# A four-layer vision network on one core: the first layer's group norm and layer norm move to the scalar engine, its input comes in channels first, and the gates' silu is spread

## The chip, the cores and the metric

The kernel runs on one core of a Trainium2 chip. A core has a matrix engine (TensorE, PE in the profile), a vector engine (VectorE, DVE), a scalar engine (ScalarE, ACT), GpSimd (POOL), and SyncE (SP), whose queue issues the DMAs here. Each engine works through its own list of instructions in order and waits on semaphores for the others. The metric is the device time of one execution in microseconds; it was 7655.37 us, the median of three runs (7653.72 to 7661.91).

## The reference, cut to what matters

Four images of 64 x 64 tokens with 128 channels pass through four residual layers. The change touches only the first, a selective scan in four directions over a group-normalized image.

```python
x = x + _L0_conv_ref(_gn(x), ...)          # the changed layer; three more follow

def _ss2d_forward(x, ...):                 # x is group-normalized, B x 64 x 64 x 128
    xz = x @ in_proj_w.T
    xh, z = jnp.split(xz, 2, axis=-1)      # 256 channels each
    z = jax.nn.silu(z)                     # the gate
    xc = conv_general_dilated(transpose(xh), conv_w, 'SAME', feature_group_count=DI)   # depthwise 3 x 3
    xc = jax.nn.silu(xc + conv_b)
    xs = the image row by row, column by column, and both reversed      # K = 4 directions
    delta, Bs, Cs = ...                    # small projections of xs
    h = exp(delta * A) * h + (delta * u) * B     # per channel and per state n = 0..15, along 4096 tokens
    y = sum over the directions of (C * h summed over n), plus D * xs
    y = (y - mean) / sqrt(var + EPS) * out_norm_w + out_norm_b          # layer norm over 256 channels
    return (y * z) @ out_proj_w.T
```

`_gn` is a group norm with 32 groups of 4 channels: mean and variance over the image and the 4 channels of a group.

## The kernel before, in words

**The scan loop.** `layer0` works through 128 units: 4 images (b = 0 to 3), for each 4 directions k, for each direction 8 chunks c of 512 tokens. So units 0 to 31 belong to image 0, 32 to 63 to image 1, 64 to 95 to image 2 and 96 to 127 to image 3. A unit has 16 slots, one per state n. In each of the 2048 slots

- GpSimd makes `dB = du * B` for both halves of the 256 channels (L689, one 128x1024 product; three buffers),
- ScalarE makes `dA = exp(delta * A)` twice, once for each half (L694), into PSUM (three buffers, `psx`),
- VectorE runs two scans `h = dA * h + dB` (L695),
- TensorE transposes a quarter of an older group of four states (L542: eight transposes into the single PSUM buffer `pt`), ScalarE copies that to SBUF (`hT`, L552), and TensorE multiplies it with C into `yT` (L577).

ScalarE's list in a slot is dA, (place act0), dA, (place act1), hT, (place act2). VectorE's list is (place dve), scan, scan, and what falls due of `yT`. TensorE's is the transposes of this slot, the products of the slot before, then one side step. These four engines keep the order that the Python code writes (`manual_schedule`); SP's DMAs are placed by the framework.

**What a unit does besides.** In fixed slots (`TABLE`) it prepares the next unit: x projections and their copies `xd` and `Ct` (slot 7), `delta` by Exp and Ln on ScalarE and one VectorE operation (slots 8 and 10), `du` on GpSimd twice. Near slots 5 and 7 `y` is added up (L593), with `ln_st` statistics in direction 2.

**The side work.** Two generators are cut into steps by `yield`, and the loop takes a step when its due time has come and the slot number is in `SIDE[need]`; `SPACE` keeps the side path free for so many slots afterwards. `later(place, f, slots=n)` queues a piece for a place n slots on.

- `before(b)` prepares the next image while the current one is scanned. For each of 8 chunks it loads 512 tokens (`l`), transposes them on TensorE (`m`, L317) and takes `bn_stats` on VectorE from PSUM (L318). After `group_scale` it loads each chunk again, transposes it again (`x`, L336), and VectorE writes the normalized values `x * s + o` from PSUM into a padded tile `xn` of 10 rows of 66 (L635 through `later`): 8 rows for this chunk, and one row each for the neighbours' borders. GpSimd clears the borders (L182, L322, L332). Then follow two gates (`z`: a product on TensorE, L177, and a silu), and, one chunk behind, two convolutions of nine taps (`c`, L159), one tap in each slot from 11 on to slot 3 of the next unit.
- `after(b)` finishes an image while the next is scanned (for image 3, in its own last units). For each of 8 chunks: load y and z, `ln_mv` on VectorE (L389), ln of the variance on ScalarE, then at step `n` the factor `nb` (L396) and four VectorE operations `normed` of 128x256 in the next slot (L423); two steps `m` with four transposes each (L404) and ScalarE's copy `yg` with the norm's weights; at `g` the product with z on GpSimd (L412); the output projection (L417), and the residual on VectorE (L426).
- `silu` is Exp, Ln(1+e), Exp on ScalarE, then one product on VectorE and a store (L358, L359). For a convolution the three are one slot apart; for a gate all three are in one slot (act0, act1, act2) and the product comes in the next.

`rest` finishes the two last chunks of image 0's convolutions in the first units, and `opening` prepares image 0. The small PSUM tiles of the side work share one bank (`spare`).

Of the kernel before, what the change touches and what calls it, by code (L numbers as in the profile page):

```python
# [11 lines left out]
F32 = mybir.dt.float32  # L12
AF = mybir.ActivationFunctionType
ALU = mybir.AluOpType
# [3 lines left out]
P = 128  # L18
# [3 lines left out]
DM = 128  # L22
NJ = NT // P
CH = 512
NCH = NT // CH
K4 = 4
WD = 32 * 129 * 16
NS = 16
# [54 lines left out]
def layer0(sh, A, x_in, x_out, scr, ahead):  # L83
# [7 lines left out]
    with ExitStack() as ctx:  # L91
# [57 lines left out]
            nc.vector.tensor_tensor(tap, tap, w_in[:, s : s + 1, :].to_broadcast([P, 9, P]), ALU.mult)  # L149
        tiles = lambda ap: ap.rearrange("(q p) d -> p q d", p=P)  # L150

        def conv(xn, s, bank):
# [13 lines left out]
            return pm  # L166
# [6 lines left out]
        def gates(b, c, v, bank, later, es=(None, None)):  # L173
            for s in range(2):
                yield "z"
                zp = bank("zp")
                nc.tensor.matmul(zp, lhsT=w_in[:, 2 + s, :], rhs=v, start=True, stop=True)  # L177
                silu(zp, 0.0, 0.0, scr(f"z{b % 3}")[s, :, c * CH : (c + 1) * CH], later, (("act1", 1), ("act2", 1), 2), es[s])

        def rows():  # L180
            xn = tmp.tile([P, 10, 66], F32, name="xn", bufs=3)
# [3 lines left out]
        def opening(bank, steps):  # L185
# [49 lines left out]
            scaled = []  # L235
# [32 lines left out]
            for c in range(DENSE + 1):  # L268
                if c < DENSE:
                    if c + 2 < NCH:  # L270
                        scale(c + 2)
                    xn = padded(c)
                    pm = psy.tile([P, 2, 2 * P], F32, name=f"yT{c % 2}").rearrange("p r d -> p (r d)")
                    acc = depthwise(c)
                if last:
                    grown(0, c - 1, 0, last[0], soon, pair("e")[:, 0], gathers[0])
                    grown(0, c - 1, 1, last[1][:, 0], soon, last[1][:, 1], gathers[1])
                if c < DENSE:
                    for _ in gates(0, c, xg[:, 8 * c : 8 * c + 8], bank, soon):
                        pass  # L280
                    for _ in conv(xn, 0, lambda name: pm):
# [16 lines left out]
        def rest(tiles, bank, later):  # L298

            for c, xn in enumerate(tiles, DENSE):  # L300
                for s in range(2):
                    pm = yield from conv(xn, s, bank)
                    grown(0, c, s, pm, later)

        def before(b, bank, later):

            st = small.tile([P, NCH, 6], F32, name="gn_st")
            for c in range(NCH):  # L310
                yield "l"
                t = tmp.tile([P, 4, DM], F32, name="xs", tag="t2", bufs=4)
                nc.sync.dma_start(t, tiles(x_in(b)[c * CH : (c + 1) * CH, :]))
                yield "m"
                pt = bank("gn_ps")
                for q in range(4):
                    nc.tensor.transpose(pt[:, q * P : (q + 1) * P], t[:, q, :], sh.ident)  # L317
                later("dve", lambda c=c, pt=pt: nc.vector.bn_stats(st[:, c, :], pt))  # L318
            yield "m"
            s_, o_ = sh.group_scale(st, psm, small, "m", exp_rstd)  # L320
            xn, ahead = None, rows()
            nc.gpsimd.memset(ahead[:, 0, :], 0.0)  # L322
            for c in range(NCH + 1):
                behind, xn = xn, ahead
                if c < NCH:
                    yield "l"
                    t = tmp.tile([P, 4, DM], F32, name="xt", tag="t2", bufs=4)
                    nc.sync.dma_start(t, tiles(x_in(b)[c * CH : (c + 1) * CH, :]))
                    if c < NCH - 1:
                        ahead = rows()  # L330
                    else:
                        nc.gpsimd.memset(xn[:, 9, :], 0.0)  # L332
                    yield "x"
                    pt = bank("x_ps")
                    for q in range(4):
                        nc.tensor.transpose(pt[:, q * P : (q + 1) * P], t[:, q, :], sh.ident)  # L336
                    grid = pt.rearrange("p (h w) -> p h w", w=64)
                    parts = [(xn[:, 1:9, 1:65], grid)]
                    if c > 0:
                        parts.append((behind[:, 9:10, 1:65], grid[:, 0:1]))  # L340
                    if c < NCH - 1:
                        parts.append((ahead[:, 0:1, 1:65], grid[:, 7:8]))
                    for dst, src in parts:
                        later("dve", nc.vector.tensor_scalar, dst, src, s_, o_, ALU.mult, ALU.add)
                    yield from gates(b, c, xn[:, 1:9, 1:65], bank, later)
                if c == 0:
                    continue
                for s in range(2):
                    pm = yield from conv(behind, s, bank)
                    grown(b, c - 1, s, pm, later)  # L350

        def silu(v, bias, minus, dst, later, wait, e=None):

# [21 lines left out]
        def after(b, st, later, bands):  # L375

            for c in bands:
# [14 lines left out]
                later("act1", nc.scalar.activation, rs, mv[:, :, 1], AF.Ln, bias=sh.eps5)  # L392
                yield "n"

                nb = spare("nb")[:, 0:4]
                nc.scalar.activation(nb, rs, AF.Exp, scale=-0.5)  # L396
                for q in range(4):
                    later("dve", normed, y[:, q, :], mv[:, q, 0:1], nb[:, q : q + 1])
                yg = tmp.tile([P, 2, CH], F32, name="yg", bufs=2)
                for s in range(2):  # L400
                    yield "m"
# [20 lines left out]
        def normed(y, mean, factor):  # L422
            nc.vector.scalar_tensor_tensor(y, y, mean, factor.to_broadcast([P, 2 * P]), ALU.subtract, ALU.mult)  # L423

        def residual(b, rows, xr, op):
            nc.vector.tensor_tensor(xr, xr, op, ALU.add)  # L426
# [128 lines left out]
        def products(G, q, hT):  # L555
# [64 lines left out]
            m={0, 1, 2, 4, 5, 11, 12, 13, 14, 15},  # L620
            x={0, 1, 4, 5, 11, 12, 13, 14, 15},
            n={0, 1, 2, 3, 4, 11, 12, 14, 15},
            z={0, 1, 2, 3, 4, 11, 12, 13, 14, 15},
            c={11},
            g={7},
            f=(),
            l=(),
        )
        SPACE = dict(m=1, x=1, n=1, z=2, c=3, g=0)
        todo = {}  # L630
        slot = 0

        def later(place, f, *a, slots=1, **kw):

            todo.setdefault((slot + slots, place), []).append(lambda: f(*a, **kw))  # L635
# [3 lines left out]
                f()  # L639

        def flush_all():
            for at in range(slot, slot + 6):
                for place in ("dve", "act0", "act1", "act2"):
                    flush(place, at)

        with tc.manual_schedule(engines=order):
            idle = lambda: None
            left = opening(any_bank, [idle, fetched, idle, begun, grown_steps, readied])
            u, ready, bd, Wd, Bb = (got[n] for n in ("u", "ready", "bd", "Wd", "Bb"))
            sides.append(Side(rest(left, spare, later), 18 * len(left), 0, 2 * NS * len(left)))  # L650
            for i, (b, k, c) in enumerate(units):
                if i % per == 0:
                    ln_st = small.tile([P, NJ, 1, 6], F32, name="ln_st")
                    first = len(left) if b == 0 else 0
                    if b + 1 < NB:
                        sides.insert(len(sides) if b == 0 else 0, Side(before(b + 1, spare, later), 17 + 8 * 22, NS * (i + first), (28 - first) * NS))
                first_out = i > 0 and rev
                rev = k >= 2
                pos = orders[b].index(k)
# [17 lines left out]
                for n in range(NS):  # L677
# [52 lines left out]

                    inside = [d for d in sides if d.inside]
                    free = not inside and slot >= taken
                    for d in inside or [d for d in sides if free and n in SIDE[d.need] and d.due(slot)][:1]:
                        taken = slot + SPACE[d.need]
                        d.free_at = slot + 1
                        d.step()
                    for d in sides:
                        if d.need in ("f", "l") and d.due(slot):
                            if d.need == "l":
                                d.free_at = slot + 3  # L740
                            d.step()
# [35 lines left out]
class Side:  # L777


    def __init__(self, pieces, count, first, slots, loads=()):  # L780
        self.pieces, self.count, self.first, self.slots, self.loads = pieces, count, first, slots, list(loads)
        self.done, self.run, self.free_at = 0, 0, first
        self.need = next(pieces)

    @property
# [1295 lines left out]
def lay_out(i):  # L2081
# [94 lines left out]
    a["proj_w"] = i["L3_conv_proj_w"].T  # L2176
    a["proj_b"] = i["L3_conv_proj_b"]
    a["x"] = i["x"].reshape(4, NT, DM)
    return {k: np.ascontiguousarray(v) for k, v in a.items()}


# [14 lines left out]
```

## Time and profile before

| what | value |
|---|---|
| median of three runs | 7655.37 us |
| the profiled execution's own time | 7655.2 us |
| its span in the profile | 7653.4 us |
| end of the first layer's last dB | 5609 us |
| mean granted TensorE clock | 0.967 |
| in the whole span: DVE, PE, ACT, POOL busy | 88%, 82%, 80%, 74% |
| DMA: queue 1's share of 16 engines | 50.6% |

The page lists busy time per engine, a picture of the span in 40 slices, the chain of work that ended last, and groups of instructions by line with the mean time of one. A group's mean is the latency of an instruction[...]; the next instruction of the same engine starts earlier than that. In the timeline, which lists instructions by their start, the distance between two starts is what an instruction costs its engine. Both kinds of number are used below, and the text says which.

The groups that the change concerns, between 100 and 5500 us (count, busy us, mean ns): VectorE `xn` 128x512 (24, 19.0, 790), `xn` 128x64 (42, 12.7, 338), `yf` 128x256, which is `normed` (112, 45.7, 472), `gn_st` (24, 16.2, 675), the gates' product `e<-zp` (52, 35.7, 687); ScalarE `xw` (52, 61.4, 1181), `e<-e` (200, 126.2, 631), `e<-zp` (48, 29.4, 612), `yg` (56, 43.6, 779).

### The profile page before, as it was taken

Reading aid. Unit: us, or ns where it says so; the run is one execution under the profiler, and the core shown is the slowest. Engines: PE = TensorE matmul, PEld = TensorE weight load, DVE = VectorE, ACT = ScalarE, POOL = GpSimd, SP = SyncE. Lnnn points to the kernel's source line nnn. Section 1 sums busy time; section 2 is a strip of 40 time slices with the busy share of each in tenths; the row PEclk is TensorE's granted clock in tenths of the full one; section 3 lists DMA queues with packets and bytes.
Section 4 is the critical chain, followed back from the end, with each engine's and each line's share of the span. In section 5 each row is a group of like instructions: output and inputs, shape, how many; then the busy total and the mean of one; then the engine's idle time right before and its main releaser. Section 6 shows DMA issues by size and latency. Waiting matters only on the chain.

```text
span 7653.4 us, 140855 instructions
## 1 busy us (share of the span) xinstructions
PE 6305.5 (82%) x52796; PEld 3991.3 (52%) x52796; DVE 6749.9 (88%) x8113; ACT 6088.5 (80%) x9683; POOL 5689.7 (74%) x2718
## 2 busy tenths in 40 slices
PE   7888888888889877888887777787789978686789
PEld 3544444444455544445554444454467756564556
DVE  7999999999999999999999999999966646656678
ACT  7999999999999999999999999999842323314667
POOL 4999999999999999999999999999920024123233
PEclk8999999999999999999999999999999979788999
DMA  5656566655666655565666445554533241231332
GB/s 171 179 172 176 179 174 175 172 171 170 192 178 179 188 187 177 158 187 179 179 186 189 168 170 180 180 184 170 185 99 73 57 113 54 77 105 43 103 99 80
DMA packets 1325854, 1158.86 MB, mean 151 GB/s; under 512 B 694133, under 2 KB 1119697, under 8 KB 1258226
## 3 DMA queue, kind: packets, MB, share of 16 engines
q1 hardware_dynamic: 1320898, 1147.43, 50.6%
q8 instruction: 416, 6.82, 0.4%
q10 hardware_dynamic: 4272, 2.43, 0.1%
q14 instruction: 268, 2.20, 0.1%
HBM read 956.37 MB, written 189.21 MB: 150 GB/s over the span
## 4 chain that ended last, share of the span: by engine, by line
ACT 35%; PE 33%; DVE 18%; issue 8%; POOL 3%; DMA 2%; SPq 1%; ACTq 0%; DVEq 0%; POOLq 0%
ACT hT L552 13%; ACT dA L694 13%; DVE h L695 11%; PE pt L542 6%; PE cv L159 5%; PE yT L577 3%; POOL dB L689 2%; ACT e L635 2%; PE pf L922 2%; PE po L935 1%; ACT delta L471 1%; PE pz L1166 1%; PE pt L1875 1%; ACT delta L474 1%; PE pu L1166 1%
## 5 line engine op out<-in xcount | busy, mean ns | idle before, releaser
L695 DVE TENSOR_TENSOR_SCAN h<-dA,state,dB 128x512 f32<-128x512 f32 x4096 | 4930.1, 1270 | 96.9 <-ACT dA L694 41.4
L689 POOL TENSOR_TENSOR dB<-du,Bb 128x1024 f32<-128x1024 f32 x2048 | 4813.5, 2389 | 153.4 <-DVE h L695 119.7
L542 PE MATMUL pt<-ident,h 128*128 128x128 f32 x16384 | 2215.0, 278 | 826.8 <-ACT hT L552 799.3
L694 ACT ACTIVATE dA<-delta,A_neg 128x512 f32<-128x512 f32 x4096 | 2752.8, 695 | 111.7 <-DVE h L695 91.2
L542 PEld LDWEIGHTS pt<-ident,h 128*128 128x128 f32 x16384 | 1806.9, 141 | 1862.5 <-ACT hT L552 1629.2
L552 ACT COPY hT<-pt 128x1024 f32<-128x1024 f32 x2048 | 2078.0, 1015 | 163.0 <-PE pt L542 143.1
L577 PE MATMUL yT<-hT,W 128*32 128x256 f32 x16384 | 1378.4, 409 | 0.4
L577 PEld LDWEIGHTS yT<-hT,W 128*32 128x32 f32 x16384 | 456.2, 151 | 342.0 <-issue 325.5
L159 PE MATMUL cv<-xn,taps 128*128 128x512 f32 x936 | 527.0, 644 | 2.5 <-DVE delta L477 2.5
L1166 POOL TENSOR_TENSOR xg<-xg,so 128x1024 f32<-128x1024 f32 x16 | 39.3, 2467 | 621.5 <-PE pu L1166 620.9
L1913 POOL TENSOR_TENSOR S<-S,sm 128x784 f32<-128x784 f32 x128 | 191.1, 1493 | 413.5 <-DVE sm L1911 239.6
L480 POOL TENSOR_TENSOR du<-delta,u 128x512 f32<-128x512 f32 x256 | 328.2, 1282 | 163.7 <-DVE delta L477 159.2
L468 PE MATMUL dp<-xd,w_dt 65*128 65x512 f32 x512 | 288.7, 646 | 40.3 <-DVE delta L477 29.4
L451 PE MATMUL yT<-u,w_x 128*48 128x512 f32 x508 | 245.3, 606 | 27.1 <-DVE y L593 26.5
L1920 ACT ACTIVATE S<-S,mx 128x196 f32<-128x196 f32 x512 | 227.9, 448 | 32.4 <-DVE mx L1947 31.8
L159 PEld LDWEIGHTS cv<-xn,taps 128*128 128x128 f32 x936 | 139.2, 188 | 179.9 <-issue 163.1
L923 ACT ACTIVATE h<-pf,b 128x512 f32<-128x512 f32 x128 | 87.6, 686 | 118.8 <-PE pf L922 100.8
L477 DVE SCALAR_TENSOR_TENSOR delta<-delta,dp 128x512 f32<-128x512 f32 x256 | 170.6, 667 | 2.5 <-ACT delta L474 1.0
L1166 POOL TENSOR_TENSOR WX<-wr,Xs 128x544 f32<-128x544 f32 x40 | 59.2, 1479 | 148.2 <-issue 63.2
L1875 PE MATMUL pt<-ident,S 128*98 128x128 f32 x1024 | 164.7, 285 | 3.4 <-POOL S L1913 2.0
L474 ACT ACTIVATE delta<-delta 128x512 f32<-128x512 f32 x256 | 164.6, 644 | 0.0
L471 ACT ACTIVATE delta<-dp 128x512 f32<-128x512 f32 x256 | 152.3, 595 | 11.7 <-PE dp L468 11.1
(381 smaller groups left out, 6937.3 us busy)
## 6 DMA issues: line engine op xcount, KB each, us to landing
Bb<-l_B SPq DMA_DIRECT2D x512, 1024.0 KB
W<-l_W SPq DMA_DIRECT2D x512, 256.0 KB
l_y<-y SPq DMA_DIRECT2D x127, 512.0 KB
u<-l_xr SPq DMA_DIRECT2D x64, 512.0 KB
u<-l_xw SPq DMA_DIRECT2D x64, 512.0 KB
y<-l_y SPq DMA_DIRECT2D x56, 512.0 KB
V<-l_v SPq DMA_DIRECT2D x512, 49.0 KB
y<-l_y SPq DMA_DIRECT2D x80, 256.0 KB
```

Of the source, the lines that this page charges most:

```text
L159: nc.tensor.matmul(pm, lhsT=taps[:, s, t, :], rhs=xn[:, dy : dy + 8, dx : dx + 64], start=(t == 0), stop=(t == 8),)
L451: nc.tensor.matmul(bank["x"], lhsT=w_x[:, s, k, :], rhs=u[:, s, :], start=(s == 0), stop=(s == 1))
L468: nc.tensor.matmul(bank[s], lhsT=w_dt[:, k, s * P : (s + 1) * P], rhs=xd, start=True, stop=True)
L480: nc.gpsimd.tensor_tensor(du[:, s, :], delta[:, s, :], u[:, s, :], ALU.mult)
L542: nc.tensor.transpose(pt[:, j, s, :], G["h"][:, s, t0 : t0 + 32, :].rearrange("p t n -> p (t n)"), sh.ident)
L552: return lambda: nc.scalar.copy(hT, pt.rearrange("p j s d -> p j (s d)"))
L577: nc.tensor.matmul(U["yT"][e][32 * jo : 32 * jo + 32, qo % 2, :], lhsT=U["Ws"][G["g"]][:, :, 4 * q + j], rhs=hT[:, j, :], start=((e, jo) n ...
L689: nc.gpsimd.tensor_tensor(dB, du, B_now[:, q : q + 1, :].to_broadcast([P, 2, CH]), ALU.mult)
L694: nc.scalar.activation(dA, delta[:, s, :], AF.Exp, scale=A_neg[:, k, s, n : n + 1])
L695: nc.vector.tensor_tensor_scan(h[:, s, :, q], dA, dB[:, s, :], state[:, s, n : n + 1], ALU.mult, ALU.add)
L1166: r = f(*args, **kw)
L1875: nc.tensor.transpose(pt[:, half, hp, :], U["S"][:, e, hp, 98 * half : 98 * half + 98], sh.ident)
```

## The change

The host lays the input out a second time, channels first and padded by one zero row and column on each side: `x_t` is 4 x 128 x 66 x 66. With it

- `before` takes its statistics from SBUF, straight from a DMA of `x_t` (8 rows of 64, in pieces of 256 bytes); the transposes of both passes are gone;
- a chunk's padded tile `xn` (10 rows of 66) comes whole in one DMA, so that GpSimd's border clearing and the one-chunk lag between gates and convolutions are gone; ScalarE applies `x * s + o` in place on the inner part, at act2, queued at the second tap of the second convolution of the chunk before;
- `normed` becomes ScalarE's `y * nb + mb`, four operations of 128x256 at act2 in four slots that follow, with one small VectorE operation for `mb = -mean * nb`;
- a gate's three ScalarE steps are one slot apart (all at act0), and its product comes four slots after the step instead of two; gates start only in slots 13 and 1, and keep the side path for four slots;
- statistics (`s`) and step `n` run beside the taps; `n` waits for a tap run while taps are still due, and is spaced by four slots; image 1's preparation may start in unit 0.

```diff
-                silu(zp, 0.0, 0.0, scr(f"z{b % 3}")[...], later, (("act1", 1), ("act2", 1), 2), es[s])
+                silu(zp, 0.0, 0.0, scr(f"z{b % 3}")[...], later, (("act0", 2), ("act0", 3), 4), es[s])
...
-                t = tmp.tile([P, 4, DM], F32, name="xs", tag="t2", bufs=4)
-                nc.sync.dma_start(t, tiles(x_in(b)[c * CH : (c + 1) * CH, :]))
-                yield "m"
-                pt = bank("gn_ps")
-                for q in range(4):
-                    nc.tensor.transpose(pt[:, q * P : (q + 1) * P], t[:, q, :], sh.ident)
-                later("dve", lambda c=c, pt=pt: nc.vector.bn_stats(st[:, c, :], pt))
+                t = tmp.tile([P, CH], F32, name="xs", tag="t2", bufs=4)
+                nc.sync.dma_start(t.rearrange("p (h w) -> p h w", w=64), A["x_t"][b, :, 8 * c + 1 : 8 * c + 9, 1:65])
+                yield "s"
+                later("dve", nc.vector.bn_stats, st[:, c, :], t)
...
-                    pt = bank("x_ps")
-                    for q in range(4):
-                        nc.tensor.transpose(pt[:, q * P : (q + 1) * P], t[:, q, :], sh.ident)
-                    grid = pt.rearrange("p (h w) -> p h w", w=64)
-                    parts = [(xn[:, 1:9, 1:65], grid)]
...
-                    for dst, src in parts:
-                        later("dve", nc.vector.tensor_scalar, dst, src, s_, o_, ALU.mult, ALU.add)
+            def load(c):
+                xn = tmp.tile([P, 10, 66], F32, name="xn", bufs=3)
+                nc.sync.dma_start(xn, A["x_t"][b, :, 8 * c : 8 * c + 10, :])
+                return xn
+
+            def scaled(xn, c, r0, r1):
+                inner = xn[:, max(r0, int(c == 0)) : min(r1, 10 - int(c == NCH - 1)), 1:65]
+                nc.scalar.activation(inner, inner, AF.Identity, scale=s_, bias=o_)
...
+                for s in range(2):
+                    for t, piece in enumerate(conv(xn, s, bank, out := [])):
+                        yield piece
+                        if c < NCH - 1 and (s, t) == (0, 0):
+                            ahead = load(c + 1)
+                        if c < NCH - 1 and s == 1 and t == 1:
+                            later("act2", scaled, ahead, c + 1, 0, 10)
+                    grown(b, c, s, out[0], later)
...
-                nb = spare("nb")[:, 0:4]
+                nb = small.tile([P, 4], F32, name="nb")
                 nc.scalar.activation(nb, rs, AF.Exp, scale=-0.5)
+                mb = small.tile([P, 4], F32, name="mb")
+                later("dve", nc.vector.scalar_tensor_tensor, mb, mv[:, :, 0], -1.0, nb, ALU.mult, ALU.mult)
                 for q in range(4):
-                    later("dve", normed, y[:, q, :], mv[:, q, 0:1], nb[:, q : q + 1])
+                    norm = dict(scale=nb[:, q : q + 1], bias=mb[:, q : q + 1])
+                    later("act2", nc.scalar.activation, y[:, q, :], y[:, q, :], AF.Identity, slots=1 + q // 1, **norm)
...
-            z={0, 1, 2, 3, 4, 11, 12, 13, 14, 15},
+            z={13, 1},
             c={11},
             g={7},
+            s={11, 12, 13, 14, 15, 0, 1, 2, 3},
...
-        SPACE = dict(m=1, x=1, n=1, z=2, c=3, g=0)
+        SPACE = dict(m=1, x=1, n=1, z=4, c=3, g=0)
...
+                        if d.need == "s" and n in SIDE["s"] and d.due(slot):
+                            d.step()
+                        if d.need == "n" and n in SIDE["n"] and d.due(slot) and (inside or not any(o.taps for o in sides)):
+                            d.free_at = slot + 4
+                            d.step()
...
+    a["x_t"] = np.pad(i["x"].reshape(4, 64, 64, DM).transpose(0, 3, 1, 2), ((0, 0), (0, 0), (1, 1), (1, 1)))
```

In the changed program's order of instructions, the scan loop has 66 `xn` and 124 `normed` operations less on VectorE and 31 `mb` more, 24 `xn` and 123 `yf` operations more on ScalarE, 30 memsets less on GpSimd, and 192 transposes of 128x128 less on TensorE. The number of loads stays (48 in the loop).

More of the change, by code (lines that the diff above doesn't have):

```diff
@@ L150, in layer0, with conv @@
         tiles = lambda ap: ap.rearrange("(q p) d -> p q d", p=P)
-        def conv(xn, s, bank):
+        def conv(xn, s, bank, out):
             for t in range(9):
@@ L165, in conv @@
                 )
-            return pm
+            out.append(pm)
         def grown(b, c, s, pm, later, e=None, gather=None):
@@ L177, in gates @@
                 nc.tensor.matmul(zp, lhsT=w_in[:, 2 + s, :], rhs=v, start=True, stop=True)
-                silu(zp, 0.0, 0.0, scr(f"z{b % 3}")[s, :, c * CH : (c + 1) * CH], later, (("act1", 1), ("act2", 1), 2), es[s])
+                silu(zp, 0.0, 0.0, scr(f"z{b % 3}")[s, :, c * CH : (c + 1) * CH], later, (("act0", 2), ("act0", 3), 4), es[s])
         def rows():
@@ L280, in opening @@
                         pass
-                    for _ in conv(xn, 0, lambda name: pm):
+                    for _ in conv(xn, 0, lambda name: pm, []):
                         pass
@@ L301, in rest @@
                 for s in range(2):
-                    pm = yield from conv(xn, s, bank)
-                    grown(0, c, s, pm, later)
+                    yield from conv(xn, s, bank, out := [])
+                    grown(0, c, s, out[0], later)
         def before(b, bank, later):
@@ L319, in before @@
+                nc.sync.dma_start(t.rearrange("p (h w) -> p h w", w=64), A["x_t"][b, :, 8 * c + 1 : 8 * c + 9, 1:65])
+                yield "s"
+                later("dve", nc.vector.bn_stats, st[:, c, :], t)
             yield "m"
             s_, o_ = sh.group_scale(st, psm, small, "m", exp_rstd)
[L321 to L333, printed above, removed]
-                    pt = bank("x_ps")
-                    for q in range(4):
-                        nc.tensor.transpose(pt[:, q * P : (q + 1) * P], t[:, q, :], sh.ident)
-                    grid = pt.rearrange("p (h w) -> p h w", w=64)
-                    parts = [(xn[:, 1:9, 1:65], grid)]
[L339 to L342, printed above, removed]
-                    for dst, src in parts:
-                        later("dve", nc.vector.tensor_scalar, dst, src, s_, o_, ALU.mult, ALU.add)
-                    yield from gates(b, c, xn[:, 1:9, 1:65], bank, later)
-                if c == 0:
-                    continue
-                for s in range(2):
-                    pm = yield from conv(behind, s, bank)
-                    grown(b, c - 1, s, pm, later)
@@ new lines, in load @@
+            def load(c):
[5 more added lines that the diff above has]
+                nc.scalar.activation(inner, inner, AF.Identity, scale=s_, bias=o_)
+            yield "l"
+            ahead = load(0)
+            yield "x"
+            later("act2", scaled, ahead, 0, 0, 10)
@@ new lines, in before @@
+            for c in range(NCH):
+                xn = ahead
+                yield from gates(b, c, xn[:, 1:9, 1:65], bank, later)
+                for s in range(2):
+                    for t, piece in enumerate(conv(xn, s, bank, out := [])):
[5 more added lines that the diff above has]
+                    grown(b, c, s, out[0], later)
@@ L420, in after @@
                 later("dve", residual, b, rows, xr, op, slots=2)
-        def normed(y, mean, factor):
-            nc.vector.scalar_tensor_tensor(y, y, mean, factor.to_broadcast([P, 2 * P]), ALU.subtract, ALU.mult)
         def residual(b, rows, xr, op):
@@ L641, in flush_all @@
         def flush_all():
-            for at in range(slot, slot + 6):
+            for at in range(slot, slot + 12):
                 for place in ("dve", "act0", "act1", "act2"):
@@ L649, in layer0 @@
             u, ready, bd, Wd, Bb = (got[n] for n in ("u", "ready", "bd", "Wd", "Bb"))
-            sides.append(Side(rest(left, spare, later), 18 * len(left), 0, 2 * NS * len(left)))
+            sides.append(Side(rest(left, spare, later), 18 * len(left), 0, 2 * NS * len(left), taps=True))
             for i, (b, k, c) in enumerate(units):
@@ L653, in layer0 @@
                     ln_st = small.tile([P, NJ, 1, 6], F32, name="ln_st")
-                    first = len(left) if b == 0 else 0
+                    first = 0
                     if b + 1 < NB:
-                        sides.insert(len(sides) if b == 0 else 0, Side(before(b + 1, spare, later), 17 + 8 * 22, NS * (i + first), (28 - first) * NS))
+                        sides.insert(len(sides) if b == 0 else 0, Side(before(b + 1, spare, later), 19 + 8 * 20, NS * (i + first), (27 - first) * NS, taps=True))
                 first_out = i > 0 and rev
@@ L732, in layer0 @@
                     free = not inside and slot >= taken
-                    for d in inside or [d for d in sides if free and n in SIDE[d.need] and d.due(slot)][:1]:
+                    for d in inside or [d for d in sides if free and d.need not in ("n", "s") and n in SIDE[d.need] and d.due(slot)][:1]:
                         taken = slot + SPACE[d.need]
@@ L777, with __init__ @@
 class Side:
-    def __init__(self, pieces, count, first, slots, loads=()):
+    def __init__(self, pieces, count, first, slots, loads=(), taps=False):
         self.pieces, self.count, self.first, self.slots, self.loads = pieces, count, first, slots, list(loads)
-        self.done, self.run, self.free_at = 0, 0, first
+        self.done, self.run, self.free_at, self.taps = 0, 0, first, taps
         self.need = next(pieces)
```

## The prediction

> **What bounds the kernel now.** I read the page's 40 slices first, then the engines' waits from 100 to 5500 us (the scan loop), then the timeline slot by slot.
>
> ```profile
> PE   7888888888889877888887777787789978686789
> DVE  7999999999999999999999999999966646656678
> ACT  7999999999999999999999999999842323314667
> POOL 4999999999999999999999999999920024123233
> ```
> ```profile
> 100.00:5500.00 5400.00, 4477.82 (x35469) 2648.97 (x35470) 5284.52 (x5069) 5078.00 (x7300) 5093.68 (x2336) 0.99 0.59 178
> ```
> ```profile
> DVE h L695 <- ACT dA L694: 41.1, 111, 0.9
> DVE h L695 <- POOL dB L689: 26.9, 32, 5.3
> ```
>
> The change lies in the first 29 slices. There VectorE is busy 5284.5 of 5400 us (97.9%), GpSimd 94.3% and ScalarE 94.0%: one engine is full, and two stand 4% behind. VectorE waits little, for dA and for dB. So what leaves VectorE is worth time, until one of the other two takes over.
>
> The price of a slot, from starts in the timeline: a scan costs 1.175 us (14.12 us for twelve below, 847.04 to 861.16), so a slot of two scans 2.35. ScalarE's dA, dA, hT cost 0.61 + 0.61 + 0.90 = 2.12, GpSimd's dB 2.34 (three in 7.01, below). TensorE allows a slot every 2.25 us without a tap, every 2.53 with one (888.01, 890.54, 893.07: ScalarE waits 0.31 for `pt` each time). Any other VectorE operation comes on top of 2.35. In the timeline of VectorE, with an `xn` step and both gates of a chunk:
>
> ```profile
> 834.64 1.29 DVE L635 TENSOR_SCALAR xn<-x_ps,gn_s,gn_o 128x512 f32<-128x512 f32 x3
> 835.85 4.80 DVE L695 TENSOR_TENSOR_SCAN h<-dA,state,dB 128x512 f32<-128x512 f32 x4
> 840.61 0.69 DVE L358 SCALAR_TENSOR_TENSOR e<-zp,e 128x512 f32<-128x512 f32 x1
> 841.26 4.81 DVE L695 TENSOR_TENSOR_SCAN h<-dA,state,dB 128x512 f32<-128x512 f32 x4
> 846.41 0.69 DVE L358 SCALAR_TENSOR_TENSOR e<-zp,e 128x512 f32<-128x512 f32 x1 [0.34 <-ACT e L635]
> 847.04 14.21 DVE L695 TENSOR_TENSOR_SCAN h<-dA,state,dB 128x512 f32<-128x512 f32 x12
> ```
>
> `xn` costs 1.21 us (834.64 to 835.85) and nothing covers it; scans stand end to end before and after it. The gates' ScalarE triples cost VectorE only the 0.34 shown and about 0.25 more: while VectorE did `xn`, ScalarE ran ahead by two dA, and this lead paid for the triples. That lead is what the change spends. At the end of a tap run it is used up, in the timeline of ScalarE and of VectorE:
>
> ```profile
> 893.07 1.01 ACT L552 COPY hT<-pt 128x1024 f32<-128x1024 f32 x1 [0.31 <-PE pt L542]
> 893.98 1.31 ACT L694 ACTIVATE dA<-delta,A_neg 128x512 f32<-128x512 f32 x2
> ...
> 896.51 0.70 ACT L694 ACTIVATE dA<-delta,A_neg 128x512 f32<-128x512 f32 x1
> 897.20 0.69 ACT L635 ACTIVATE e<-cv,conv_nb 128x512 f32<-128x512 f32 x1
> ```
> ```profile
> 900.11 2.46 DVE L695 TENSOR_TENSOR_SCAN h<-dA,state,dB 128x512 f32<-128x512 f32 x2 [0.31 <-ACT dA L694]
> ```
>
> One Exp of 0.6 us between two dA, with no VectorE extra beside it, and that slot lasts 2.81 instead of 2.35. Last, GpSimd, in image 3's units:
>
> ```profile
> 4394.83 2.37 POOL L412 TENSOR_TENSOR yg<-yg,zf 128x1024 f32<-128x1024 f32 x1
> 4397.16 7.05 POOL L689 TENSOR_TENSOR dB<-du,Bb 128x1024 f32<-128x1024 f32 x3
> ```
> ```profile
> 4399.56 2.47 DVE L695 TENSOR_TENSOR_SCAN h<-dA,state,dB 128x512 f32<-128x512 f32 x2 [1.13 <-POOL dB L689]
> ...
> 4413.73 7.16 DVE L695 TENSOR_TENSOR_SCAN h<-dA,state,dB 128x512 f32<-128x512 f32 x6 [0.25 <-POOL dB L689]
> 4420.81 1.63 DVE L423 SCALAR_TENSOR_TENSOR yf<-yf,ln_mv,nb 128x256 f32<-128x256 f32 x4
> 4422.36 5.98 DVE L695 TENSOR_TENSOR_SCAN h<-dA,state,dB 128x512 f32<-128x512 f32 x5
> ```
>
> A `yg` of 2.33 puts GpSimd behind, and VectorE waits 1.13. The four `yf` (1.55 us) then let GpSimd catch up. A unit asks GpSimd for 16 x 2.34 + 2 x 1.24 = 39.9 us, with `yg` 42.2; VectorE's plain unit is 37.6 + 2.3 (two `delta`, two `y`, 0.58 each) = 39.9. There is no slack between them there.
>
> **The skill beside the trace.** Perfetto Trace Analysis, "Optimizing Scalar/DVE Operations", says that with VectorE saturated it may make sense to hand work to ScalarE. The trace has the condition (97.9%), but the receiver is at 94.0%; I go by the slots. ScalarE: Activation LUTs, "Rules for kernel authors", prices an ACTIVATE at about 0.3 us plus 0.83 ns an element. The trace agrees in slope: copies from PSUM of 512 and 1024 elements take 585 and 1015 ns, 0.84 an element. An `e<-e` of 512 costs 0.52 us from start to start, so my estimates for what the trace lacks are 0.52 - 256 x 0.83 ns = 0.31 for a `yf` and 0.52 + 128 x 0.83 ns = 0.63 for a whole `xn`.
>
> **Part by part** (counts from the program's order; "+" is slower).
>
> 1. `xn` leaves VectorE: 24 of 128x512 at 0.70 and 42 of 128x64 at 0.25 (1.21 is one and two): **-27**.
> 2. `normed` leaves: 31 pieces in the loop at 1.55 are -48; `mb`, 128x4, is new: the nearest row, `ln_mv`, takes 0.15, so at 0.1 each +3. **-45**. The first 8 pieces run beside image 1, 8 beside image 2, 8 beside image 3, 7 in the last units.
> 3. Statistics: the same 24 `bn_stats` (0.60). Eight of them now lie in image 1's tap runs, where TensorE sets 2.53 and VectorE has up to 0.18 a slot free: **-4**. Those of images 2 and 3 meet no taps, 0. Transposes gone: TensorE wasn't last where they stood, 0 (to -5).
> 4. `xn` on ScalarE, 24 x 0.63, 21 of them in slot 13 together with `xw` (0.93). Such a slot with `xw` alone already runs 2.73 to 2.75, no lead left; `xn` behind it then shows for about 0.5 (after it TensorE is less behind): **+11** (0 to 15).
> 5. The gates spread: triples in 48 slots become 96 Ln and Exp in slots with no VectorE extra. ScalarE's slot is then 2.12 + 0.52 = 2.64, 0.29 over VectorE's. The triples now cost 0.6 a chunk with the `xw` of that slot; afterwards I count `xw` 0.37, the first pair 0.5, the second 0.15, together 1.0. +0.4 x 24: **+10** (-12, all of their present cost, to +37, all 96 at 0.52 less that).
> 6. `yf` on ScalarE: 123 slots of 2.12 + 0.31 = 2.43. In tap slots TensorE's 2.53 hides it, except once where it moves dA; elsewhere 0.08 each. Its wait for `mb` holds dA behind it, but `mb` stands ahead of the scans of that slot. The `m` transposes now wait for ScalarE's `yf`, with the next `pt` behind them: 0.1 to 0.3 a piece. Together **+10** (0 to 38, every `yf` in full).
> 7. GpSimd's lost lead. Beside image 3, `yf` gave it 1.55 and the next `yg` took it: of 8 x 1.45 gained I give back 8 x 1.1; beside images 1 and 2, 16 x 0.2. **+12** (0 to 35, all gained in those 24 pieces). In the last 7 pieces `yg` blocks GpSimd until ScalarE's copy is done, before and after: nothing given back. Memsets gone: 30 x 0.14, within the error.
> 8. DMA: as many loads. `xs` in 256-byte pieces is twice the pieces. Its user is now VectorE, in order, where scans would wait behind it; but it is at least four slots, 9.4 us, behind the issue, and the loop shows no VectorE wait on a DMA: 0 (to +10). On SP the load stands where the old one stood. The `xn` load comes a whole unit ahead.
> 9. Tail: one `yf`, half the transposes and one projection of the seventh piece, with a `yg` of 2.3, move behind the last scan: **+3** (-1 to +6).
>
> Sum: -27 - 45 - 4 + 11 + 10 + 10 + 12 + 3 = **-30**. The profiled execution took 7655.2 us, span 7653.4 and 1.8 around it, the median 7655.4. So 7655 - 30 = **7625 us**.
>
> **Rivals.**
>
> - *Everything hides* (4 to 7 cost nothing): -27 - 45 - 4 + 3 = -73, 7582. For it: in the loop ScalarE waits 131 us for `pt`, mostly in tap slots, where most `yf` go. Against it: the slot of 2.81.
> - *GpSimd takes over*: item 7 at its end, 35 instead of 12: -7, 7648, no change. For it: 39.9 against 39.9 in plain units, and the 1.13 wait. Against it: beside images 1 and 2 units last 42 to 45 us, and the end of a dB lies 2 to 4 us ahead of its scan.
> - *ScalarE ends every slot*: dA stands in line behind each new ACTIVATE, and with no VectorE extra beside it each shows in full, as the 0.93 of `xw` partly and the Exp of 2.81 nearly do. Items 4 to 6 at their upper ends, 15 + 37 + 38 = 90 instead of 31: +29, 7684, slower. It decides once 61 of these 90 us show: then the gain is gone. Against it: tap slots have 0.31 free, and leads are regained at slots 5 to 10.
> - *The change doesn't do what it says*: the order shows all 24 and 123 operations moved, none in a burst at an image's end; dropped.
>
> **How the numbers follow.** Partly paid for (7625, by itself 7600 to 7650) 0.50; everything hides 0.20; GpSimd 0.17; ScalarE 0.13. About 0.2%, 15 us, is what a measurement of this kernel tells from no change. Faster, under 7640: 0.46 + 0.20 + 0.03 = 0.69. Same: 0.04 + 0.12 + 0.02 = 0.18. Slower, over 7670: 0.02 + 0.11 = 0.13. The range 7580 to 7665 takes in the first three and leaves out most of the fourth.
>
> **What would show it.** In the changed profile: slots that held three `xn` or four `yf` (3.56 and 3.90 us) at 2.35 to 2.5; the slot with `xw` and `xn` at 3.2 (2.35 if it hides, 3.4 if not at all); VectorE's waits for dA up from 41 to about 70 and for dB from 27 to about 40 us; VectorE's busy share at 97%, ScalarE's at 95 to 96%. Waits for dA over 130 would mean the slower rival, waits for dB over 60 the GpSimd one. A VectorE wait of several us on `xs` would make item 8 wrong.

## The result, and the profile after

The changed kernel is slower: 7694.23 us (median of four runs, 7685.0 to 7702.05) against 7656.95 us for the kernel before, measured beside it; the ratio is 1.0048, with a 95% interval of 1.003 to 1.0065. That is 37 us more where 30 us less were forecast, and it lies outside the forecast's range. The profiled execution has a span of 7693.2 us.

The page's picture in 40 slices, for the same four engines as before:

```profile
PE   7888888778889877889887777777779978686789
DVE  7999999999999999999999999999956646656678
ACT  7999999999999999999999999999843323314667
POOL 4999999999999999999999999999820024123233
```

and the busy time by engine from 100 to 5500 us (PE, PEld, DVE, ACT, POOL, each with its count; then TensorE's clock, the DMA share and GB/s), with VectorE's two largest waits and ScalarE's for `mb`, from the view of waits over the same stretch:

```profile
100.00:5500.00 5400.00, 4454.11 (x35137) 2619.00 (x35136) 5248.76 (x4891) 5122.77 (x7409) 5075.97 (x2296) 0.99 0.59 177
```
```profile
DVE h L688 <- ACT dA L687: 76.9, 157, 1.1
...
ACT yf L628 <- DVE mb L628: 36.4, 26, 4.0
...
DVE h L688 <- POOL dB L682: 31.7, 62, 4.0
```

Nearly all the signs that the prediction named came out: VectorE's busy share is 5248.8 of 5400, 97.2% (97% forecast), ScalarE's 94.9% (95 to 96%), waits for dA 77 us (about 70; over 130 would have meant ScalarE at the end of every slot), waits for dB 32 us (about 40). None of VectorE's rows shows the loss; ScalarE's wait for `mb`, 36.4 us in 26 times, is a hint of it. From the first scan to the end of the last the loop takes 5523.5 us instead of 5499.6, though 74 us of `xn` and `normed` have left VectorE (27 and 47, from start to start). The time is inside VectorE's *busy* time, in one tiny operation that the prediction had priced at 0.1 us. In the list of VectorE's groups from 100 to 5500 us it stands fourth (busy us, mean ns, idle before):

```profile
L628 DVE SCALAR_TENSOR_TENSOR mb<-ln_mv,nb 128x4 f32<-128x4 f32 x28 | 61.3, 2188 | 0.0
```

and the view of the tile `mb` gives the spread (duration in ns, min/median/max; first and last start in us):

```profile
L628 DVE SCALAR_TENSOR_TENSOR mb<-ln_mv,nb x32: 161/2016/4558, 1690.6 to 5667.1; 128x4 f32<-128x4 f32 x32
```

An operation on four elements a partition takes 2.0 us in the median and 4.6 at most. The only one at 161 ns stands at 5667.1 us, behind the last scan, when GpSimd is idle. In the timelines of VectorE and of GpSimd, a usual one:

```profile
5337.15 2.02 DVE L628 SCALAR_TENSOR_TENSOR mb<-ln_mv,nb 128x4 f32<-128x4 f32 x1
```
```profile
5336.78 4.69 POOL L682 TENSOR_TENSOR dB<-du,Bb 128x1024 f32<-128x1024 f32 x2
```

The first of these two dB ends at 5339.15, `mb` at 5339.17. And one of the longest:

```profile
4407.65 7.16 DVE L688 TENSOR_TENSOR_SCAN h<-dA,state,dB 128x512 f32<-128x512 f32 x6 [0.27 <-POOL dB L682]
4414.73 4.54 DVE L628 SCALAR_TENSOR_TENSOR mb<-ln_mv,nb 128x4 f32<-128x4 f32 x1
4419.19 5.97 DVE L688 TENSOR_TENSOR_SCAN h<-dA,state,dB 128x512 f32<-128x512 f32 x5
```
```profile
4407.59 11.66 POOL L682 TENSOR_TENSOR dB<-du,Bb 128x1024 f32<-128x1024 f32 x5
4421.78 2.38 POOL L682 TENSOR_TENSOR dB<-du,Bb 128x1024 f32<-128x1024 f32 x1 [2.54 <-DVE h L688]
```

This `mb` begins at 4414.73, 0.14 us behind the start of the fourth dB of the row, and ends at 4419.27, with the fifth: 4407.59 + 11.66 = 4419.25. It has waited for two. Record by record, all 31 `mb` of the loop end 0.02 us behind the end of a dB: 26 of the dB that was running when they began, and 5, which began less than 0.3 us behind a dB's start, of the one after it. Why these five let a second dB go first stays open. From start to start the 31 take 63.2 us, 2.04 each, where 3 in all were forecast.

### The profile page after: what moved, and what is told of

Its sections match the earlier page's. It is cut to its first block, busy times and chain, and to the rows that moved or that the text cites. A ratio compares the mean times of both kernels' runs of the same rounds, so it can differ in the third digit from the quotient of the medians.

```text
span 7693.2 us, 140355 instructions
## 1 busy us (share of the span) xinstructions
PE 6306.8 (82%) x52604; PEld 3976.1 (52%) x52604; DVE 6737.2 (88%) x7951; ACT 6160.7 (80%) x9835; POOL 5693.1 (74%) x2688
## 4 chain that ended last, share of the span: by engine, by line
ACT 36%; PE 31%; DVE 18%; issue 7%; POOL 3%; DMA 2%; SPq 1%; ACTq 0%; DVEq 0%; POOLq 0%
ACT hT L544 14%; ACT dA L687 14%; DVE h L688 11%; PE pt L534 6%; PE cv L159 4%; PE yT L569 3%; POOL dB L682 3%; ACT e L628 2%; PE pf L920 2%; PE po L933 1%; ACT delta L463 1%; PE pt L1873 1%; ACT delta L466 1%; PE pu L1164 1%; PE pa L1164 1%
## 5 line engine op out<-in xcount | busy, mean ns | idle before, releaser
L1164 DVE TENSOR_TENSOR WX<-wr,Xs 128x544 f32<-128x544 f32 x88 | 78.2, 906 | 99.1 <-PE pz L1164 66.7
```

Of the source, the lines that this page charges most:

```text
L1164: r = f(*args, **kw)
```

## The experiments

Ratios and differences to the kernel before are against its own runs beside each experiment (medians of 7657.5 to 7659.1 us). Diffs show the lines that matter.

**Theory 1**: `mb` reads two tensors in SBUF (`ln_mv` and `nb`), GpSimd's dB reads SBUF too, and VectorE has to wait until a dB has ended. The Trainium skill, SBUF — State Buffer, "Who interferes with whom", says so in general: a VectorE instruction with two SBUF inputs contends with a GpSimd instruction that reads SBUF, and one with at most one such input, outside certain double-rate modes, doesn't; e11 and e12 below agree (up to 4.54 us with two, 0.16 at most with one). `normed` before had its factor in PSUM and its mean as a pointer scalar (a column of 128x1, one value a partition), so one tensor in SBUF. **Theory 2**: ScalarE ends the slots, and `mb`, which waits for ScalarE's `nb`, is only where that shows.

### One suspect at a time, in the kernel before

e11 adds the instruction alone to the kernel before; e12 is the same with one operand elsewhere.

```diff
+                mb = small.tile([P, 4], F32, name="mb")
+                later("dve", nc.vector.scalar_tensor_tensor, mb, mv[:, :, 0], -1.0, rs, ALU.mult, ALU.mult)   # e11
+                later("dve", nc.vector.scalar_tensor_tensor, mb, mv[:, :, 0], -1.0, nb, ALU.mult, ALU.mult)   # e12, instead
                 for q in range(4):
                     later("dve", normed, y[:, q, :], mv[:, q, 0:1], nb[:, q : q + 1])
```

> The kernel before plus one instruction a piece: the 128x4 scalar_tensor_tensor mb, ahead of the four normed, with the mean and ln_r as its two tensor operands, both in SBUF; nothing reads mb. Nothing else of the change is in it, ScalarE's work is that of before. Theory 1: each mb lasts as long as the running dB still needs, 31 x 1 to 2.4 us = 31 to 74 us, so 7690 to 7730 us. Theory 2 (ScalarE): 31 x 0.1 = 3 us, 7656 to 7662 us.

> As e11, the same instruction in the same place and of the same size, but its second tensor operand is nb, which lies in PSUM in the kernel before. Theory 1: one tensor operand in SBUF waits for nobody: mb at 0.16 us, 31 x 0.1 = 3 us, 7656 to 7664 us. If it is the instruction or its place, not the operand's: as e11.

e11: 7721.12 us, ratio 1.0077 (1.006 to 1.0093), +62 us. e12: 7656.56 us, ratio 0.9998 (0.9989 to 1.0007), no difference. The tile view of each:

```profile
L637 DVE SCALAR_TENSOR_TENSOR mb<-ln_mv,ln_r x32: 135/1124/4544, 1533.5 to 5697.6; 128x4 f32<-128x4 f32 x32
```
```profile
L637 DVE SCALAR_TENSOR_TENSOR mb<-ln_mv,nb x32: 125/130/158, 1533.8 to 5631.8; 128x4 f32<-128x4 f32 x32
```

The instruction, its size and its place are the same; only where the second operand lies differs. In PSUM it takes 130 ns, though a GpSimd operation is running beside 28 of the 32, and costs nothing that can be measured; in SBUF up to 4.5 us. Of e11's 31 in the loop, the 29 that meet a dB end within 0.03 us of the end of one, and the two that meet none take 0.14 us each. ScalarE's work is that of before in both. The loop of e11 is 65 us longer, its records of `mb` add up to 53; the cause of the other 12 us stays open.

e3 puts the factor of the old `normed` into SBUF, one line in the kernel before:

```diff
-                nb = spare("nb")[:, 0:4]
+                nb = small.tile([P, 4], F32, name="nb")
```

> The kernel before, with one line changed: nb lies in SBUF instead of PSUM, so each of the four normed (128x256) of a piece has two tensor operands in SBUF; the order of instructions is unchanged. Theory 1: each normed waits for a dB to end or holds the next one up, 0.5 to 2.3 us each, 124 in the loop: +60 to +290 us, 7715 to 7945 us, and yf well over its 0.47 us. Theory 2: operand places do not matter, 7652 to 7660 us.

7770.7 us (two runs), ratio 1.0148 (1.013 to 1.0167), +112 us for the same instructions in the same order. In the timelines of VectorE and GpSimd, one piece of four `normed`, which took 1.63 us before:

```profile
5457.58 5.56 DVE L423 SCALAR_TENSOR_TENSOR yf<-yf,ln_mv,nb 128x256 f32<-128x256 f32 x4
```
```profile
5457.24 4.83 POOL L689 TENSOR_TENSOR dB<-du,Bb 128x1024 f32<-128x1024 f32 x2
```

The first waits out the dB in progress (2.29 us), the next dB begins before the first has ended, the second waits for that (2.56 us), and the last two take 0.47 each. So it is in 25 of the 31 pieces in the loop; in the other 6 the first outlasts two dB (3.36 to 4.81 us) and the second is free. Since only the place of `nb` differs from the kernel before, it isn't a matter of the instruction that writes the operand either.

### The change with `mb` made in another way

e1 makes `mb` by four operations with one tensor operand each, e2 on ScalarE.

```diff
-                later("dve", nc.vector.scalar_tensor_tensor, mb, mv[:, :, 0], -1.0, nb, ALU.mult, ALU.mult)
+                for q in range(4):                                     # e1
+                    later("dve", nc.vector.tensor_scalar, mb[:, q : q + 1], mv[:, q, 0:1], nb[:, q : q + 1], -1.0, ALU.mult, ALU.mult)
...
+                minus = small.tile([P, 4], F32, name="minus")          # e2
+                nc.scalar.activation(minus, nb, AF.Identity, scale=-1.0)
+                for q in range(4):
+                    nc.scalar.activation(mb[:, q : q + 1], mv[:, q, 0:1], AF.Identity, scale=minus[:, q : q + 1])
```

> As the changed kernel, but mb is made by four VectorE tensor_scalar of 128x1, each with the mean as its one tensor operand and nb as a pointer scalar, in the same slot and behind the same wait. Theory 1 (mb, with two tensor operands in SBUF, waits until GpSimd's dB, which also reads SBUF, is done: 65.7 us of records, 60.6 us of stretched slots): a small operation that reads one tensor waits for nobody; four at 0.06 to 0.15 us are 31 x 0.24 to 0.6 = 7 to 19 us, so 7694 - 61 + 7 to 19 = 7640 to 7652 us, and no mb over 0.3 us. Theory 2 (ScalarE ends the slots; mb is only the place where its delay shows, since mb waits for nb): 7690 to 7705 us, and the first of the four is as long as mb was.

> As the changed kernel, but mb is made on ScalarE: -nb by one ACTIVATE of 128x4 and four of 128x1, nothing on VectorE. Theory 1: the 61 us are gone; five small ACTIVATEs at 0.1 to 0.25 us start to start are 0.5 to 1.25 us a piece of which a part shows: 7635 to 7665 us. Theory 2: more on ScalarE, so 7700 to 7730 us.

e1: 7644.43 us, ratio 0.9982 (0.9976 to 0.9989). Its tile view and waits:

```profile
L629 DVE TENSOR_SCALAR mb<-ln_mv,nb x128: 187/206/232, 1691.4 to 5623.1; 128x1 f32<-128x1 f32 x128
```
```profile
DVE h L689 <- ACT dA L688: 81.9, 175, 1.1
DVE h L689 <- POOL dB L683: 31.3, 50, 3.8
```

No `mb` over 0.23 us, though a GpSimd operation runs beside 123 of the 128; the four cost 0.47 us together from start to start. The loop falls from 5523.5 to 5478.9 us, 44.6 less: 63.2 less 31 x 0.47 is 48.6, and VectorE's other waits give 4 back. The waits for dA and dB are nearly those of the changed kernel, so these weren't what made it slow. Theory 2 falls for the loss. e2: 7675.84 us, ratio 1.0023 (1.0014 to 1.0032), 31 us above e1: the five small ACTIVATEs and `nb` before them cost ScalarE about 1.1 us more a piece, 34 us for 31 pieces, and that shows in full or more, since VectorE does 15 us less. It lies between what the two theories said (7665 at most, 7700 at least). For ScalarE as a limit on what is given to it, theory 2 has a point.

### What the parts are worth without the stall

e8 is the changed kernel with the whole layer norm as before: group norm and gates alone.

```diff
-                yield "n"
+                yield "v"                       # free slots, as n before
...
-                nb = small.tile([P, 4], F32, name="nb")
+                nb = spare("nb")[:, 0:4]
...
+                    later("dve", normed, y[:, q, :], mv[:, q, 0:1], nb[:, q : q + 1])
```

> The changed kernel with the whole layer norm as before (factor in PSUM, normed on VectorE, old slots); what is left of the change is the group norm with its input laid out channels first, and the spread gates. Forecast's items 1, 3, 4 and 5: -27 - 4 + 11 + 10 = -10, 7649 us. With xn in slot 13 at what e1 shows (about 20 instead of 11): 7656 to 7660 us. Rival (the gain of the change is all in the group norm, the layer norm gives nothing even with mb cured): as e1 or below, 7635 to 7645 us.

7645.74 us, ratio 0.9983 (0.9977 to 0.999), the same as e1: group norm and gates are worth 13 us, and the layer norm's move, even with `mb` cured, nothing. In the profile e1's loop is 5.9 us shorter than e8's (5478.9 against 5484.8), and from the end of the last scan to the first projection of the next layer it takes 43.0 us against 32.2: what the loop gains, the tail takes. The stretches of each profiled execution, in us:

| | before | changed | e1 | e8 | e5 |
|---|---|---|---|---|---|
| first to last scan | 5499.6 | 5523.5 | 5478.9 | 5484.8 | 5479.3 |
| last scan to next layer | 32.6 | 42.9 | 43.0 | 32.2 | 32.6 |
| from there to the end (unchanged layers) | 2009.3 | 2014.4 | 2011.3 | 2007.0 | 2010.6 |
| VectorE's waits for dA, 100 to 5500 us | 41.1 | 76.9 | 81.9 | 66.5 | 79.7 |

The third row is the same code in all kernels; over all the profiled executions of this record it runs from 2007.0 to 2021.0 us. A difference of a few us between two medians can come from there, so the first two rows tell more of the change.

e5 undoes the move for the last image only (`on_dve = b == NB - 1`, else as e1).

> As e1, but the layer norm of the last image (b = 3, eight pieces) is done as in the kernel before: factor in PSUM, four normed on VectorE, in the old slots. Its last units took 46.41 us each in e1 and 46.23 before, so the loop should not change by more than 1 to 2 us; between the last scan and layer 1 e1 took 42.9 us, before 32.6, since one whole yg, product and projection stand behind the last scan. If the tail is lost to the place of that piece: 7644 - 10 = 7634 us and 32 to 34 us from last scan to layer 1. If ScalarE's layer norm gains in the last units what it takes from VectorE (4 x 0.39 less four mb, 6 x 1.1 = 6.7 us): 7639 to 7645 us.

7640.52 us, ratio 0.9973 (0.9962 to 0.9984); the interval overlaps e1's, but the profile shows the step: 32.6 us instead of 43.0 from last scan to next layer, and a loop of 5479.3 against 5478.9 us. GpSimd's timeline at the end, of the changed kernel, of the kernel before and of e5:

```profile
5628.74 2.38 POOL L682 TENSOR_TENSOR dB<-du,Bb 128x1024 f32<-128x1024 f32 x1 [0.18 <-DVE h L688]
5659.15 2.34 POOL L407 TENSOR_TENSOR yg<-yg,zf 128x1024 f32<-128x1024 f32 x1 [28.04 <-ACT yg L628]
5672.81 2.34 POOL L407 TENSOR_TENSOR yg<-yg,zf 128x1024 f32<-128x1024 f32 x1 [11.32 <-ACT yg L628]
```
```profile
5638.14 2.34 POOL L412 TENSOR_TENSOR yg<-yg,zf 128x1024 f32<-128x1024 f32 x1 [29.17 <-ACT yg L635]
```
```profile
5619.12 2.34 POOL L411 TENSOR_TENSOR yg<-yg,zf 128x1024 f32<-128x1024 f32 x1 [29.14 <-ACT yg L636]
```

In the changed kernel two products `yg` stand behind the last scan, and each carries transposes, copies and a projection with it; in e5, as before, only one.

e4 is e1 with a gate's three ScalarE steps in one slot again:

```diff
-                silu(..., (("act0", 2), ("act0", 3), 4), es[s])
+                silu(..., (("act1", 1), ("act2", 1), 2), es[s])
...
-            z={13, 1},
+            z={0, 1, 2, 3, 4, 11, 12, 13, 14, 15},
...
-        SPACE = dict(m=1, x=1, n=1, z=4, c=3, g=0)
+        SPACE = dict(m=1, x=1, n=1, z=2, c=3, g=0)
```

> As e1 (mb by four small operations), but the gates' three ACTIVATEs stand in one slot again as in the kernel before, with its slots and spaces for z. It sizes the spread of the gates alone. The forecast's item 5 (the spread costs 10 us, between -12 and +37): e1 less 10 us. The rival, everything hides: within 4 us of e1. If the spread was worth something: e1 plus 5 to 12 us.

7664.58 us, ratio 1.0007 (1.0 to 1.0013), 20 us slower than e1. In the profile the loop accounts for 11 of them: a slot with three `e` shows 0.59 us over VectorE's own work (48 slots, 28.4 us), where it showed 0.28 or less before, with `xn` on VectorE near it. In the profiled executions the tails are alike (43.0 us) and 4 us more stand in the unchanged layers; the rest of the 20 isn't in these traces.

### Is `xn` only in the wrong slot?

In the changed kernel the slot with `xw`, `xn` and a tap is the longest regular one. The timelines of ScalarE and VectorE:

```profile
833.84 0.70 ACT L687 ACTIVATE dA<-delta,A_neg 128x512 f32<-128x512 f32 x1
834.46 1.18 ACT L362 COPY xw<-e 128x512 f32<-128x512 f32 x1
835.40 0.72 ACT L687 ACTIVATE dA<-delta,A_neg 128x512 f32<-128x512 f32 x1
836.05 1.01 ACT L544 COPY hT<-pt 128x1024 f32<-128x1024 f32 x1
836.96 0.93 ACT L326 ACTIVATE xn<-xn,gn_o,gn_s 128x640 f32<-128x640 f32 x1
837.78 1.30 ACT L687 ACTIVATE dA<-delta,A_neg 128x512 f32<-128x512 f32 x2
```
```profile
831.50 5.96 DVE L688 TENSOR_TENSOR_SCAN h<-dA,state,dB 128x512 f32<-128x512 f32 x5
838.57 9.51 DVE L688 TENSOR_TENSOR_SCAN h<-dA,state,dB 128x512 f32<-128x512 f32 x8 [1.11 <-ACT dA L687]
```

From dA to dA it is 0.62 + 0.94 + 0.65 + 0.91 + 0.82 us on ScalarE, and the scan behind it waits 1.11. So e6 (on e1) puts `xn` in slot 5, e9 (on e5) in slot 9, and e10 (on e5) two halves in slots 9 and 12; e7 is e5 and e6 together.

```diff
-                        if c < NCH - 1 and s == 1 and t == 1:
-                            later("act2", scaled, ahead, c + 1, 0, 10)
+                        if c < NCH - 1 and s == 1 and t == 8:
+                            later("act2", scaled, ahead, c + 1, 0, 10, slots=2)   # e6; slots=6 in e9
...
+                            later("act2", scaled, ahead, c + 1, 0, 5, slots=6)    # e10
+                            later("act2", scaled, ahead, c + 1, 5, 10, slots=9)
```

> As e1, but the xn of the next chunk (group norm, 128x640 on ScalarE) stands in slot 5, a plain slot behind the run of taps, instead of slot 13 together with xw and a tap. In e1 the 21 slots with xw, xn and a tap are 1.20 us over VectorE's price each, those with xw alone 0.35 before. Forecast's view (xn costs because xw and a tap are in its slot): 21 x (1.20 - 0.35 - 0.1 to 0.5 for xn alone) = 7 to 16 us gained, 7628 to 7637 us. Rival (ScalarE has no slack anywhere, so xn costs its 0.8 us wherever it stands): 7640 to 7648 us.

> e5 and e6 together. If their gains are independent: the sum of both against e1, some 7618 to 7630 us, 0.4 to 0.5% below the kernel before. If one is hidden by the other: no better than the better of the two.

> As e5, but xn in slot 9, which has no gates and one delta (0.58 us) on VectorE as a cover, instead of slot 13. e6 moved it to slot 5, where an e of the gates turned out to stand: that slot kept 0.34 of xn and the tap slots behind gained 8 us. If xn needs a slot with a VectorE extra: 21 x 0.85 = 17 us gained less 0 to 5, 7623 to 7629 us against e5's 7640. If ScalarE has too little slack in the whole unit (16 slots of 2.12, delta 2.1, e 1.6, copies 1: some 38.6 of 39.9 us), the 0.8 us shows in later slots: 7636 to 7645 us.

> As e5, but xn in two ACTIVATEs of 128x320 (about 0.55 us each from start to start), in slots 9 and 12. yf, 0.5 us each in four slots in a row, showed only 0.03 to 0.17 us a slot, so halves should hide better than one whole although ScalarE does 0.3 us more: if the size of one piece decides, 7622 to 7630 us; if ScalarE's whole work in the unit decides, 7640 to 7650 us, worse than e9.

| run | median us | ratio, 95% interval | loop, first to last scan |
|---|---|---|---|
| e6 | 7654.03 | 0.9993 (0.9985 to 1.0001) | 5482.1, e1 5478.9 |
| e7 | 7644.90 | 0.9983 (0.9977 to 0.999) | 5485.2, e5 5479.3 |
| e9 | 7651.37 | 0.9993 (0.9984 to 1.0001) | 5489.5, e5 5479.3 |
| e10 | 7652.22 | 0.9993 (0.9985 to 1.0001) | 5490.0, e5 5479.3 |

No place is better than slot 13; all are 3 to 11 us worse in the loop. (e6's median stands further off, 9.6 us above e1's; its profiled execution spends 2019.6 us in the unchanged layers, e1's 2011.3.) The slot with `xw` alone falls back to 0.30 us as hoped, but a whole `xn` shows 0.34 to 0.5 in most slots where it goes (e6, e9), and the 401 tap slots without another ScalarE piece become 0.020 us longer each, 8 us in all. Why those do stays open. My view that slot 13 is to blame is refuted: `xn` costs at least its own 0.82 us in every place tried, about 0.87 in slot 13 (item 4 below) and by the loop 0.16 to 0.51 more for each of the 21 moved. e5 is the fastest version found.

## Why the prediction was wrong

**The step that failed is item 2**: "`mb`, 128x4, is new: the nearest row, `ln_mv`, takes 0.15, so at 0.1 each +3". It measured 2.04 us each from start to start, 63.2 us in 31 slots, since it waited for dB to end. `ln_mv` was the nearest row by size, but not by operands: it reads one tensor in SBUF. The kernel before had the sign in its names: every recurring operation of two tensors on VectorE in its loop has one of them in PSUM (dA of the scan, `yT` of `y`, `dp` of `delta`, `zp` and `cv` of `e`, `op` of `xr`, `nb` of `yf`), and the change gave that place up for `nb`. With 63 in place of 3 the forecast's own sum is +30; with the tail as measured (item 9 below) +37, against +37. So close a fit is partly luck: of the 39.7 us between the two profiled executions the loop holds 23.9, the tail 10.3 and the unchanged layers 5.1, and items 3 and 4 below miss by 7 and 10 in opposite directions. Item 2 also gave `mb` no upper bound, so neither the range nor a rival held this: the rival "ScalarE ends every slot" gave 7684 us by another mechanism, and its own sign, waits for dA over 130 us, didn't come (77).

The other items, with e1 and e8 as the change without the stall. Waits below are the length of a slot, from scan start to scan start, less 1.175 us for each scan and the start-to-start cost of VectorE's other operations in it, summed over the loop by what ScalarE has in the slot:

- **Items 1 and 2, what leaves VectorE**: right. With the four `mb` of e1 VectorE's own work in the loop falls by about 60 us (27 for `xn`, 47 for `yf`, 15 back for `mb`). In e1 the waits between its operations rise from 194 to 236 us, by 42; items 3 to 7 had 39 for them, which fits in part because their errors cancel.
- **Item 3**: too small, -11 instead of -4. Plain tap slots show 0.098 us over VectorE's work before and 0.074 in e8, 43.5 against 32.6 us in 442 and 441 slots; the transposes gone from TensorE and the statistics in those slots weren't told apart.
- **Item 4, `xn`**: +11 forecast, about +21 measured: 34.5 us in slots with `xw` or `xn` in e1 (without those that hold `yg` or a gate too) against 13.6 in slots with `xw` before. It hid nothing: the slot with `xw`, `xn` and a tap lasts 3.53 us, where the prediction had 3.2, or 3.4 if nothing hides. One costs 0.82 us, not the 0.63 that the prediction scaled from `e`. A `yf` costs 0.50, not 0.31. The price that the Trainium skill states (ScalarE: Activation LUTs, "Rules for kernel authors": 0.3 us, with the bias in a pointer column, and 0.83 ns an element) gives 0.83 and 0.51, which agrees with both; my shift by the 0.52 of `e`, which has no pointer column, was wrong.
- **Item 5, gates**: +10 forecast, about +8 measured against before (59 us in slots with `e`, 51 before). e4 shows that leaving the three together would have cost more; that their cover went with `xn` fits this, but no run separates it.
- **Items 6 and 7, `yf` on ScalarE and GpSimd's lead**: 22 forecast, about 26 measured, between e8 and e1. The division was off: "in the last 7 pieces nothing given back" is wrong. Units 122 to 126 take 46.41 us in e1 and 46.2 before, though VectorE has 1.06 us less in each.
- **Item 8**: right; no wait of VectorE for `xs` is among the waits.
- **Item 9, tail**: +3 forecast, +10.3 measured (32.6 to 42.9 us). The seventh piece's `yg`, its copies and its projection aren't overlapped with the eighth's: the two `yg` stand 13.7 us apart.

## What to carry to other kernels

Price a new VectorE operation by where its tensor operands lie, not by its size: with two of them in SBUF beside a GpSimd stream that reads SBUF, four elements cost 2 us; with one in PSUM 0.13, and with one as a pointer scalar 0.12 an operation from start to start. An engine that stands still in this way counts as busy, so look for a small instruction whose maximum is many times its minimum. And before work is moved from a full engine to one at 94%, ask for the places where the receiver's time is really free: here the layer norm's move, with the stall cured, came out even, and `xn` cost at least its own time in every slot tried.

## What the runs showed of the hardware

- Each operation of a row waits anew: in e3, 25 of 31 second `normed` waited for a dB that had begun while the first was still under way (2.56 us, dB being 2.34).
- The wait can take in more than the dB that is running: 5 of 31 `mb` in the changed kernel and 6 of 31 in e11 ended only with the dB after it (3.1 to 4.6 us).
- VectorE's `tensor_scalar` of 128x1 with a pointer scalar took 0.21 us in e1, never longer than 0.23, with GpSimd at work beside 123 of 128.
- ScalarE's in-place ACTIVATE with two pointer columns cost 0.50 us for 256 elements, an `e<-e` with constants 0.52 for 512. Other rows fit a price of about 0.1 us for a pointer column: the same Exp of 128x512 from PSUM costs 0.58 with one (`e<-cv,conv_nb`, 897.20 to 897.78 in the kernel before) and 0.49 without (`e<-zp`, 843.22 to 843.71). On the prediction's own estimates, 0.31 + 2 x 0.1 and 0.63 + 2 x 0.1 come near the 0.50 of a `yf` and the 0.82 of an `xn`. No run changed this alone.
